# A decoder layer on one core: the value projections first, the first context's splits queued behind single units

## The chip, the cores and the metric

The kernel runs on one core of one Trainium2 chip. The metric is the device time of the whole program in microseconds (us). Before the change it is 2504.05 us, the median of three runs between 2503.03 and 2505.15.

## What is computed

One decoder layer over x (8 sequences of 100 tokens, 1024 wide) and a context of 8 x 722 vectors of 1024, all in float32:

```python
x = layernorm(x + retention(x))        # 8 heads, query/key 128, value 256, RoPE, decay, gate
x = layernorm(x + attention(x, ctx))   # 16 query heads, 4 key/value heads of 128
x = layernorm(x + ffn(x))              # SwiGLU, 4096 hidden

# attention(x, ctx): the part that the change touches
q, k, v = x @ wq, x @ wk, x @ wv                  # 16, 4 and 4 heads
q, k = rope(rms_norm(q)), rope(rms_norm(k))
k_ctx, v_ctx = rms_norm(ctx @ wk_ctx), ctx @ wv_ctx
out = softmax(q @ [k_ctx, k].T * scale + causal_mask) @ [v_ctx, v] @ wo
```

## The kernel before

**Tiles.** Activations lie with the feature on the partitions. The 800 tokens are two halves of N = 400 (four sequences each). A weight tile is 1024 x 128, held as 128 partitions x 1024. For float32 accuracy every operand is split into a high and a low part (`split2`, L60 to L68): ACT casts the high part, DVE subtracts it from the source for the low one, so each split is one ACT and one DVE instruction, both with line 68. One product is three matmuls (`mm3`, L90 high x high, L93 high x low, L94 low x high). `proj` makes one unit: 8 x 3 = 24 matmuls of 128 x 400 into one PSUM bank. There are eight banks: three with the tag "a" (projections), four "s", one "v".

**Places.** A tile gets the next place of its tag, in rotation, and waits until the tile that had it is done with. Raw weights have three places ("wst"), split weights four ("w"). `load_w` (L70 to L80) loads a raw weight (SP, L74) and splits it. `load_ws` (L82 to L85) loads a weight that was split earlier and stored (`wcd`, 1 MB, SP L84) straight into one of the same four "w" places.

**Order.** Each engine (PE, ACT, DVE, POOL, and SP, which here only issues DMAs) runs a fixed list of instructions, in which semaphores make it wait. The lists are laid out by a scheduler when the program is built, from the program's order, its dependences and a model of durations. Some things are pinned: `keep_in_program_order`, the function `todo` that `proj` calls between two of its matmul groups, and `tc.issue_after(i)`, which keeps an instruction behind instruction i on its engine.

**Stages.** Retention for eight heads; its output projection with the first layer norm (`out_proj`, "ln1"); the second projections ("l2", the changed loop); attention over eight sequences ("cx"); its output projection with the second norm; the feed-forward with the third.

**The norm ahead of the loop.** The second half's norm (`norm_late`, `inv_root`, `scaled`) is called from `todo` inside the last matmul groups of half 1's output and inside the first unit of the second projections, which uses half 0 only. Its sums over features are matmuls with a constant matrix (L291). On DVE it is: subtract (L343, L348), root (L133, L135), eight scalings (L312) and eight low parts of z (L68, z<-y,z); on ACT eight high parts of z.

**The second projections (L668 to L700).** For each kv head: units i = 0 to 3 are its four queries, 4 its key, 5 its value. Groups of a kv head are (0,4), (4,6) for the first and (0,2), (2,4), (4,6) for the others; in a group first the weights are loaded, then all units of half 0 and then those of half 1 run.

- A query or key unit: square (ACT L691), sum over partitions (POOL L140), rotation (`rope`: two ACT copies L148 and L149, three DVE products and sums L150 to L152, of which L150 reads the "a" bank), root of the mean (`inv_root`: ACT L127, L130, L132, DVE L133, L135), a DVE product (L696), a split into d (three places) and a store (SP L700, to qd or kd).
- A value unit: `tokens_first` copies the bank (ACT L160, one place "vt"), PE transposes four 100-token pieces into an "s" bank (L163), `split2` writes them into "vs" (one place) and SP stores that (L688, to vd, 100 partitions).

**The first context.** `load_context(0)` is called at the start of the second group. It loads eight pieces (SP L634, cs, into the weights' "wst" places) and splits each into two tiles with the tag "big" (ACT and DVE L68, big<-cs). The scheduler has put their splits between the instructions of the norm. `context_keys(kv)` loads a context key weight (`load_ws`) and returns `step`, which makes one half of the keys: 24 matmuls, a square, a POOL sum, a scaled copy and its low part. Steps for kv 0 and 1 run at the start of the groups (1,2), (2,0), (2,2) and (3,0); the attention's first sequence uses what they made.

Of the kernel before, what the change touches and what calls it, by code (L numbers as in the profile page):

```python
# [8 lines left out]
F32 = mybir.dt.float32  # L9
FR = mybir.dt.float32r  # L10
AF = mybir.ActivationFunctionType
ALU = mybir.AluOpType
# [4 lines left out]
P = 128  # L17
B, T, D = 8, 100, 1024
NB = 4
N = NB * T  # L20
KT = D // P
QT = KT // 2
# [9 lines left out]
NKV = 4  # L32
# [8 lines left out]
def decoder_layer(ctx, tc, xT, cT, w1, wo1, w2, wo2, wc, w3, wd, gw, qw, kw, trig, dec, mask, out):  # L41
    nc = tc.nc

    def sbuf(name, bufs, side=None):
        return tc.tile_pool(name=name, bufs=bufs, side=side, reuse_waits="tile")
# [8 lines left out]
    def bank(tag):  # L54
        return ps.tile([P, 512], F32, tag=tag, name=tag, bufs=banks[tag])

    def f32(ap):
        return ap.bitcast(F32)

    def bt(ap):  # L60
        return ap.rearrange("p (b t) -> p b t", b=NB)

    def split(dst, src):

        return split2(dst[:, 0], dst[:, 1], src)

    def split2(hi, lo, src):
        return nc.scalar.copy(hi, src), nc.vector.tensor_tensor(lo, src, f32(hi), ALU.subtract)  # L68

    def load_w(src, w=None, pinned=None):  # L70
        st = wp.tile([P, KT * P], F32, tag="wst", name="wst", bufs=3)
        if w is None:
            w = wp.tile([P, 2, KT * P], FR, tag="w", name="w", bufs=4)
        nc.sync.dma_start(out=st, in_=src)  # L74
        if pinned:
            with tc.issue_after(pinned[0].ins), tc.issue_after(pinned[1].ins):
                split(w, st)
        else:
            split(w, st)
        return w  # L80
# [32 lines left out]
    def proj(w, z, n=N, tag="a", todo=None):  # L113
        acc = bank(tag)[:, :n]
        for k in range(KT):
            pinned = between(todo, k)
            t = z[k // QT]
            mmw(acc, w, k, t[:, 0, k % QT, :n], t[:, 1, k % QT, :n], k == 0, k == KT - 1, pinned)
        return acc
# [4 lines left out]
    def inv_root(pool, ss, eps, n=N, pin=False, at=None):  # L124

        r = pool.tile([P, n], F32, tag="r0", name="r0") if at is None else at
        ln = nc.scalar.activation(r, ss, AF.Ln, bias=eps)  # L127
        if pin:
            tc.keep_in_program_order(ln)
        nc.scalar.activation(r, r, AF.Exp, scale=-0.5)  # L130
        q = pool.tile([P, n], F32, tag="r1", name="r1")
        nc.scalar.activation(q, r, AF.Square)  # L132
        nc.vector.scalar_tensor_tensor(q, ss, eps, q, ALU.add, ALU.mult)  # L133
        out = q if at is None else at
        nc.vector.scalar_tensor_tensor(out, q, 3.0, r, ALU.subtract, ALU.mult)  # L135
        return out

    def all_red(pool, x, tag, op=RED.add):
        y = pool.tile([P, N], F32, tag=tag, name=tag)
        nc.gpsimd.partition_all_reduce(y, x, P, op)  # L140
        return y

    def rope(pool, acc, cosw, sinw, tag="t1", op=ALU.add, swapped=None):

        t1 = pool.tile([P, N], F32, tag=tag, name=tag)
        t2 = pool.tile([P, N], F32, tag="t2", name="t2") if swapped is None else swapped
        h = P // 2
        nc.scalar.copy(t2[0:h], acc[h:P])  # L148
        nc.scalar.copy(t2[h:P], acc[0:h])  # L149
        nc.vector.tensor_tensor(bt(t1), bt(acc), cosw[:, None, :].to_broadcast([P, NB, T]), ALU.mult)  # L150
        nc.vector.tensor_tensor(bt(t2), bt(t2), sinw[:, None, :].to_broadcast([P, NB, T]), ALU.mult)
        nc.vector.tensor_tensor(t1, t1, t2, op)  # L152
        return t1

    def tokens_first(pool, acc, copied=True):

        vt = acc
        if copied:
            vt = pool.tile([P, N], F32, tag="vt", name="vt", bufs=1)
            nc.scalar.copy(vt, acc)  # L160
        tr = bank("s")
        for b in range(NB):
            nc.tensor.transpose(tr[0:T, b * P:(b + 1) * P], vt[:, b * T:(b + 1) * T], ident)  # L163
        return tr[0:T]
# [447 lines left out]
    with sbuf("ln1", 1) as p:  # L612
        z1, todo = [], None
        for half in range(2):
            todo, _ = out_proj(half, wo1, load_o1, xT, p, 2, p, lambda _: [
                z1p.tile([P, 2, QT, N], FR, tag="z", name="z") for _ in range(2)], zd, z1, todo)
        ws2 = [load_w(w2[0, 0])]
        acc2 = [proj(ws2[0], z1[0], todo=todo)]


# [1 line left out]
    ka = kapool.__enter__()  # L622
    cz = []

    def load_context(b):

        cz.clear()
        for hf in range(2):
            n = SN[hf]
            z = [big([P, 2, QT, SH]) for _ in range(2)]  # L630
            for k in range(0, KT, 2):
                cs = wp.tile([P, KT * P], F32, tag="wst", name="cs", bufs=3)
                cs = cs[:, :2 * n].rearrange("p (k n) -> p k n", k=2)
                nc.sync.dma_start(out=cs, in_=cT[b, :, k:k + 2, hf * SH:hf * SH + n])  # L634
                split(z[k // QT][:, :, k % QT:k % QT + 2, :n], cs)
            cz.append(z)

    def context_keys(kv):

        kall = ka.tile([P, 2, SC + T], FR, tag="kall", name="kall")  # L640
        wk = load_ws(2 * kv)
        sq = ka.tile([P, SC], F32, tag="ksq", name="ksq", bufs=1)
        ss = ka.tile([P, 6 * P], F32, tag="kss", name="kss", bufs=1)
        row = dr.tile([6, P], F32, tag="row", name="row", bufs=2)
        nc.gpsimd.memset(ss[:, SC:], 1.0)

        def step(hf):
            n, at = SN[hf], slice(hf * SH, hf * SH + SN[hf])
            acc = proj(wk, cz[hf], n)
            nc.scalar.activation(sq[:, at], acc, AF.Square)  # L650
            nc.gpsimd.partition_all_reduce(ss[:, at], sq[:, at], P, RED.add)  # L651
            nc.scalar.activation(kall[:, 0, at], acc, AF.Copy, scale=kws)
            nc.vector.scalar_tensor_tensor(kall[:, 1, at], acc, kws, f32(kall[:, 0, at]), ALU.mult, ALU.subtract)
            if hf:
                nc.sync.dma_start(out=row.rearrange("c p -> (c p)")[None, :], in_=ss[0:1])
        return step, (kall, row)
# [8 lines left out]
        return vt  # L665


    early = []  # L668
    with sbuf("l2", 2) as p:
        for kv in range(NKV):  # L670
            for i0, i1 in ((0, 4), (4, 6)) if kv == 0 else ((0, 2), (2, 4), (4, 6)):
                if (kv, i0) == (0, 4):
                    load_context(0)
                ws = [ws2.pop() if ws2 else load_w(w2[kv, i]) for i in range(i0, i1)]
                if (kv, i0) in ((1, 2), (2, 2)):
                    step, kept = context_keys(kv - 1)
                    early.append(kept)
                if (kv, i0) in ((1, 2), (2, 0), (2, 2), (3, 0)):
                    step(i0 == 0)
                for half in range(2):  # L680
                    bs = slice(half * NB, (half + 1) * NB)
                    for i in range(i0, i1):
                        acc = acc2.pop() if acc2 else proj(ws[i - i0], z1[half])
                        if i == 5:
                            tr = tokens_first(p, acc).rearrange("p (b d) -> p b d", b=NB)
                            vs = p.tile([T, NB, 2, P], FR, tag="vs", name="vs", bufs=1)
                            split2(vs[:, :, 0], vs[:, :, 1], tr)
                            nc.sync.dma_start(out=f32(vd[kv, :, bs]), in_=f32(vs))  # L688
                            continue
                        sq = p.tile([P, N], F32, tag="sq", name="sq")  # L690
                        nc.scalar.activation(sq, acc, AF.Square)  # L691
                        ss = all_red(p, sq, "ss")
                        tb = tq if i < 4 else tk
                        t = rope(p, acc, tb[:, 0], tb[:, 1], swapped=bank("s")[:, :N])
                        r = inv_root(p, ss, eps_k, at=bank("s")[:, :N])
                        nc.vector.scalar_tensor_tensor(  # L696
                            t, t, -0.5 if i < 4 else -0.5 * math.sqrt(P), r, ALU.mult, ALU.mult)
                        d = p.tile([P, NB, 2, T], FR, tag="d", name="d", bufs=3)
                        split2(d[:, :, 0], d[:, :, 1], bt(t))
                        nc.sync.dma_start(out=f32(qd[kv, i, :, bs] if i < 4 else kd[kv, :, bs]), in_=f32(d))  # L700
    z1pool.__exit__(None, None, None)


# [501 lines left out]
```

## Time and profile before

| | |
|---|---|
| median of three runs | 2504.05 us |
| profiled execution | 2504.06 us |
| its span, first to last instruction | 2502.3 us |
| granted TensorE clock, mean | 0.994 |
| PE busy | 2463.2 us (98%) |
| DVE busy | 1954.5 us (78%) |
| ACT busy | 1343.0 us (54%) |
| POOL busy | 464.8 us (19%) |

All times inside the program count from the span's start. The profile has several views: busy time of each engine in stretches of the span, with the granted clock of TensorE (1.00 is full speed) and the share that the DMA engines were busy; rows of waits (engine and line that waited, what ended the wait, total us, how often, the longest); a timeline of instructions (start, duration, engine, line, operation, output<-inputs, shape, how many in a row, and in brackets the idle time ahead of it); and the chain of work that ended last. "SPq" rows are DMAs that SP issued. The norm and the second projections lie between about 577 and 860 us.

### The profile page before, as it was taken

How to read it: one execution, taken by the hardware profiler on the slowest of the kernel's cores; microseconds unless marked ns; L12 is line 12 of the kernel's file. 1: busy time of each engine (PE TensorE's matmuls, PEld its weight loads, DVE VectorE, ACT ScalarE, POOL GpSimd, SP SyncE). 2: the span in 40 equal slices, each digit the busy share in tenths (PEclk: the TensorE clock that was granted, in tenths of full speed). 3: DMA queues.
4: the chain of work that ended last, by engine and by line, in shares of the span. 5: the costliest groups of instructions: out<-in, count | busy, mean ns of one | idle time of the engine just before them, and what ended most of it. 6: DMA issues, size and time to landing. Idle time of an engine off the chain costs nothing.

```text
span 2502.3 us, 37231 instructions
## 1 busy us (share of the span) xinstructions
PE 2463.2 (98%) x14068; PEld 2440.7 (98%) x14068; DVE 1954.5 (78%) x3101; ACT 1343.0 (54%) x2260; POOL 464.8 (19%) x234
## 2 busy tenths in 40 slices
PE   9999999997999999999999999999999999999997
PEld 9999999997999999999999999999999999999997
DVE  7778877567877688989999999866987777666756
ACT  6666676335767555656566666533544544432221
POOL 0111111002455343433433434100000000000000
PEclk9999999998999999999999999999999999999999
DMA  7333445774444654554554553574445444389731
GB/s 242 111 111 128 137 144 178 242 271 134 166 145 137 210 174 160 163 167 155 167 176 142 168 195 127 199 256 153 143 175 195 169 166 168 124 285 324 276 103 53
DMA packets 224451, 433.98 MB, mean 173 GB/s; under 512 B 47338, under 2 KB 168042, under 8 KB 211854
## 3 DMA queue, kind: packets, MB, share of 16 engines
q1 hardware_dynamic: 222542, 426.87, 50.2%
q0 software_dynamic: 1152, 4.19, 1.1%
q8 instruction: 111, 1.82, 0.3%
q14 instruction: 70, 0.57, 0.1%
q10 hardware_dynamic: 576, 0.52, 0.1%
HBM read 322.18 MB, written 109.35 MB: 172 GB/s over the span
## 4 chain that ended last, share of the span: by engine, by line
PE 93%; DVE 3%; DMA 2%; ACT 1%; issue 1%; POOL 0%; SPq 0%; DVEq 0%; ACTq 0%
PE a L94 20%; PE a L90 20%; PE a L93 20%; PE s L94 9%; PE s L93 9%; PE s L90 9%; PE v L94 2%; PE v L90 2%; PE v L93 2%; PE s L531 1%; PE s L734 1%; PE s L163 1%; DVE w L68 1%; DMA big<-o1d 1%; DVE y L312 0%
## 5 line engine op out<-in xcount | busy, mean ns | idle before, releaser
L90 PE MATMUL a<-big,w 128*128 128x400 f32 (+2 forms) x1808 | 609.5, 338 | 2.8 <-DMA w<-wcd 1.0
L93 PE MATMUL a<-big,w 128*128 128x400 f32 (+2 forms) x1808 | 609.3, 337 | 0.3 <-DVE big L68 0.3
L94 PE MATMUL a<-big,w 128*128 128x400 f32 (+2 forms) x1808 | 607.6, 337 | 0.4 <-DVE w L68 0.4
L68 ACT CAST w<-wst 128x1024 fp32r<-128x1024 f32 (+1 forms) x231 | 239.6, 1039 | 397.4 <-PE a L94 144.0
L68 DVE TENSOR_TENSOR w<-wst,w 128x1024 fp32r<-128x1024 f32 (+1 forms) x231 | 284.6, 1232 | 143.0 <-ACT w L68 141.7
L90 PEld LDWEIGHTS a<-big,w 128*128 128x128 f32 x1808 | 339.7, 188 | 5.9 <-ACT big L68 1.7
L93 PEld LDWEIGHTS a<-big,w 128*128 128x128 f32 x1808 | 340.3, 188 | 1.9 <-DVE big L68 1.0
L94 PEld LDWEIGHTS a<-big,w 128*128 128x128 f32 x1808 | 340.2, 188 | 1.2 <-DVE w L68 0.6
L90 PE MATMUL a<-z,w 128*128 128x400 f32 x680 | 236.4, 348 | 17.7 <-DVE t L150 16.0
L94 PE MATMUL a<-z,w 128*128 128x400 f32 x680 | 236.1, 348 | 0.0
L93 PE MATMUL a<-z,w 128*128 128x400 f32 x680 | 236.0, 347 | 0.0
L90 PE MATMUL s<-big,w 128*128 128x400 f32 x664 | 231.7, 349 | 2.4 <-ACT w L68 1.8
L94 PE MATMUL s<-big,w 128*128 128x400 f32 x664 | 229.9, 347 | 1.0 <-DVE w L68 1.0
L93 PE MATMUL s<-big,w 128*128 128x400 f32 x664 | 229.8, 346 | 0.0
L140 POOL PARTITION_ALL_REDUCE ss<-sq x56 | 150.7, 2693 | 328.8 <-DMA zd<-y 167.8
L651 POOL PARTITION_ALL_REDUCE kss<-ksq x64 | 166.7, 2604 | 127.8 <-ACT ksq L650 127.2
L90 PEld LDWEIGHTS a<-z,w 128*128 128x128 f32 x680 | 128.7, 189 | 19.5 <-DVE t L150 13.3
L768 ACT ACTIVATE s<-s,rk 128x400 f32<-128x400 f32 x160 | 87.9, 592 | 95.4 <-DVE sm L788 65.4
L90 PEld LDWEIGHTS s<-big,w 128*128 128x128 f32 x664 | 125.0, 188 | 5.3 <-ACT w L68 3.0
L94 PEld LDWEIGHTS a<-z,w 128*128 128x128 f32 x680 | 129.4, 190 | 0.0
L93 PEld LDWEIGHTS a<-z,w 128*128 128x128 f32 x680 | 128.7, 189 | 0.5
L94 PEld LDWEIGHTS s<-big,w 128*128 128x128 f32 x664 | 125.7, 189 | 1.7 <-DVE w L68 1.7
(356 smaller groups left out, 5443.8 us busy)
## 6 DMA issues: line engine op xcount, KB each, us to landing
wst<-in_w SPq DMA_DIRECT2D x135, 512.0 KB
w<-wcd SPq DMA_DIRECT2D x64, 1024.0 KB
wst<-in_wo SPq DMA_DIRECT2D x64, 512.0 KB
hd<-h SPq DMA_DIRECT2D x12, 1400.0 KB
wst<-in_wd SPq DMA_DIRECT2D x64, 256.0 KB
big<-o1d SPq DMA_DIRECT2D x16, 800.0 KB
qd<-d SPq DMA_DIRECT2D x32, 400.0 KB
q<-qd SPq DMA_DIRECT2D x32, 400.0 KB
```

What stands on the lines that cost most here:

```text
L68: return nc.scalar.copy(hi, src), nc.vector.tensor_tensor(lo, src, f32(hi), ALU.subtract)
L90: i = nc.tensor.matmul(acc, lh, rh, start=start, stop=False, skip_group_check=chain)
L93: nc.tensor.matmul(acc, lh, rl, start=False, stop=False, skip_group_check=chain)
L94: nc.tensor.matmul(acc, ll, rh, start=False, stop=stop, skip_group_check=chain)
L140: nc.gpsimd.partition_all_reduce(y, x, P, op)
L163: nc.tensor.transpose(tr[0:T, b * P:(b + 1) * P], vt[:, b * T:(b + 1) * T], ident)
L531: nc.tensor.matmul(bt(o)[:, b], vv[:, b * P:(b + 1) * P], pf[:, b], start=True, stop=True)
L651: nc.gpsimd.partition_all_reduce(ss[:, at], sq[:, at], P, RED.add)
L734: nc.tensor.transpose(tr[0:rows, (c - c0) * P:(c - c0 + 1) * P], vt[:, c * P:c * P + rows], ident)
L768: nc.scalar.activation(sc, sp, AF.Copy, scale=rk[:, c:c + 1])
```

## The change

- The first weight loaded is the value weight of kv head 0, not its first query's.
- The loop runs over a flat list of groups: first all four values (eight units: four with half 0, four with half 1), then for each kv head the group of queries 0 and 1 and the group of queries 2, 3 and the key.
- `load_context` becomes a generator, `context_steps`, that makes one of its eight pieces at each call. The first context's pieces are asked for one by one ahead of units 4 to 11 (counted from 0), so from the first value of half 1 on. They have two places of their own in the pool of the loop, and `issue_after` puts the split of a piece behind the split of the latest unit, on ACT and on DVE.
- The steps of the context's keys stand at the start of groups 2, 3, 5 and 7 (counted from 0).

Later contexts are loaded as before. In the built program the instruction lists of all engines are the same ahead of the norm and from the attention's first part on; between 577 and about 950 us they differ in order, with the same matmuls.

```diff
-        ws2 = [load_w(w2[0, 0])]
+        ws2 = [load_w(w2[0, 5])]
...
-    def load_context(b):
+    def context_steps(b, pool, bufs, behind=None):
...
-                cs = wp.tile([P, KT * P], F32, tag="wst", name="cs", bufs=3)
+                cs = pool.tile([P, KT * P if behind is None else 2 * SH], F32, tag="wst", name="cs", bufs=bufs)
                 cs = cs[:, :2 * n].rearrange("p (k n) -> p k n", k=2)
                 nc.sync.dma_start(out=cs, in_=cT[b, :, k:k + 2, hf * SH:hf * SH + n])
-                split(z[k // QT][:, :, k % QT:k % QT + 2, :n], cs)
-            cz.append(z)
+                to = z[k // QT][:, :, k % QT:k % QT + 2, :n]
+                if behind is None:
+                    split(to, cs)
+                else:
+                    with tc.issue_after(behind[0].ins), tc.issue_after(behind[1].ins):
+                        split(to, cs)
+                if k == 0:
+                    cz.append(z)
+                yield
+
+    def load_context(b):
+        for _ in context_steps(b, wp, 3):
+            pass
...
     early = []
+    behind = [None, None]
+    groups = [[(kv, 5) for kv in range(NKV)]]
+    for kv in range(NKV):
+        groups += [[(kv, i) for i in range(2)], [(kv, i) for i in range(2, 5)]]
+    unit = 0
     with sbuf("l2", 2) as p:
-        for kv in range(NKV):
-            for i0, i1 in ((0, 4), (4, 6)) if kv == 0 else ((0, 2), (2, 4), (4, 6)):
-                if (kv, i0) == (0, 4):
-                    load_context(0)
-                ws = [ws2.pop() if ws2 else load_w(w2[kv, i]) for i in range(i0, i1)]
-                if (kv, i0) in ((1, 2), (2, 2)):
-                    step, kept = context_keys(kv - 1)
-                    early.append(kept)
-                if (kv, i0) in ((1, 2), (2, 0), (2, 2), (3, 0)):
-                    step(i0 == 0)
+        ctx0 = context_steps(0, p, 2, behind)
+        for g, group in enumerate(groups):
+            ws = [ws2.pop() if ws2 else load_w(w2[kv, i]) for kv, i in group]
+            if g in (2, 5):
+                step, kept = context_keys(len(early))
+                early.append(kept)
+            if g in (2, 3, 5, 7):
+                step(g in (3, 7))
+            for half in range(2):
+                bs = slice(half * NB, (half + 1) * NB)
+                for (kv, i), w in zip(group, ws):
+
+                    if 4 <= unit < 12:
+                        next(ctx0)
+                    acc = acc2.pop() if acc2 else proj(w, z1[half])
+                    unit += 1
+                    if i == 5:
...
+                        behind[:] = split2(vs[:, :, 0], vs[:, :, 1], tr)
...
+                    behind[:] = split2(d[:, :, 0], d[:, :, 1], bt(t))
```

More of the change, by code (lines that the diff above doesn't have):

```diff
@@ L668, in decoder_layer @@
     early = []
-    with sbuf("l2", 2) as p:
-        for kv in range(NKV):
-            for i0, i1 in ((0, 4), (4, 6)) if kv == 0 else ((0, 2), (2, 4), (4, 6)):
-                if (kv, i0) == (0, 4):
-                    load_context(0)
-                ws = [ws2.pop() if ws2 else load_w(w2[kv, i]) for i in range(i0, i1)]
-                if (kv, i0) in ((1, 2), (2, 2)):
-                    step, kept = context_keys(kv - 1)
-                    early.append(kept)
-                if (kv, i0) in ((1, 2), (2, 0), (2, 2), (3, 0)):
-                    step(i0 == 0)
[L680 to L700, printed above, removed]
@@ new lines, in decoder_layer @@
+    behind = [None, None]
[3 more added lines that the diff above has]
+    unit = 0
+    with sbuf("l2", 2) as p:
+        ctx0 = context_steps(0, p, 2, behind)
[14 more added lines that the diff above has]
+                    if i == 5:
+                        tr = tokens_first(p, acc).rearrange("p (b d) -> p b d", b=NB)
+                        vs = p.tile([T, NB, 2, P], FR, tag="vs", name="vs", bufs=1)
+                        behind[:] = split2(vs[:, :, 0], vs[:, :, 1], tr)
+                        nc.sync.dma_start(out=f32(vd[kv, :, bs]), in_=f32(vs))
+                        continue
+                    sq = p.tile([P, N], F32, tag="sq", name="sq")
+                    nc.scalar.activation(sq, acc, AF.Square)
+                    ss = all_red(p, sq, "ss")
+                    tb = tq if i < 4 else tk
+                    t = rope(p, acc, tb[:, 0], tb[:, 1], swapped=bank("s")[:, :N])
+                    r = inv_root(p, ss, eps_k, at=bank("s")[:, :N])
+                    nc.vector.scalar_tensor_tensor(
+                        t, t, -0.5 if i < 4 else -0.5 * math.sqrt(P), r, ALU.mult, ALU.mult)
+                    d = p.tile([P, NB, 2, T], FR, tag="d", name="d", bufs=3)
+                    behind[:] = split2(d[:, :, 0], d[:, :, 1], bt(t))
+                    nc.sync.dma_start(out=f32(qd[kv, i, :, bs] if i < 4 else kd[kv, :, bs]), in_=f32(d))
```

## The prediction

> **What bounds the kernel now.** Read the page's busy shares first: PE is busy 98% of the span, the slices show one stretch with a lower digit inside the kernel (slice 10, 563 to 626 us), and the chain of waits is 93% PE. So the end moves only by what changes PE's idle time, or its clock, around the second projections. The table by stretches says where (columns: window, us, PE, PEld, DVE, ACT and POOL busy, granted clock, DMA share, GB/s).
>
> ```profile
> 580.00:600.00 20.00, 18.64 (x98) 17.42 (x96) 18.33 (x31) 11.91 (x20) 0.00 (x0) 1.00 0.53 154
> 600.00:610.00 10.00, 0.00 (x0) 0.00 (x0) 9.93 (x20) 7.42 (x15) 1.71 (x1) 0.61 0.76 275
> 610.00:620.00 10.00, 8.34 (x35) 8.30 (x36) 6.52 (x14) 5.91 (x13) 8.33 (x3) 0.71 0.00 0
> 620.00:630.00 10.00, 8.82 (x49) 8.52 (x48) 9.93 (x15) 8.62 (x17) 5.65 (x3) 1.00 0.25 91
> 630.00:640.00 10.00, 6.97 (x30) 6.60 (x30) 9.97 (x15) 7.12 (x14) 5.39 (x2) 0.83 0.52 181
> 800.00:820.00 20.00, 20.00 (x112) 20.00 (x111) 19.16 (x36) 16.92 (x35) 11.33 (x6) 1.00 0.49 158
> ```
>
> PE stands still from 598.6 to 611.7, loses 1.3 and 3.2 us more by 635.8, and runs at half clock behind two of these stops; from 640 to 860 it is full but for about 0.9 us. The wait rows name the engine, and DVE's timeline why it is late:
>
> ```profile
> PE a L90 <- DVE t L150: 16.0, 2, 13.0
> PE a L90 <- DMA w<-wcd: 1.0, 2, 0.6
> ```
> ```profile
> 603.26 3.97 DVE L312 SCALAR_TENSOR_TENSOR y<-y,r 128x400 f32<-128x400 f32 x8
> 607.15 3.97 DVE L68 TENSOR_TENSOR z<-y,z 128x400 fp32r<-128x400 f32 x8
> 611.03 0.57 DVE L150 TENSOR_TENSOR t<-a,tq 128x400 f32<-128x400 f32 x1
> ```
>
> The first query's L150 must read its "a" bank, and on DVE it stands behind the eight scalings and eight splits of the LN1 norm; all three "a" banks are held, so PE waits 13.0 us.
>
> **Part 1, gained in the norm.** The eight splits of the first context (L68, big<-cs) leave the norm for later places: 8 x 0.91 = 7.3 us of DVE between 576 and 602, some of it also waiting for ACT's half, which waits for the loads. The norm without such guests is in this trace too, in LN2: its variance matmul starts at 1739.86, its first scaling (L312) at
>
> ```profile
> 1745.10 3.98 DVE L312 SCALAR_TENSOR_TENSOR y<-y,r 128x400 f32<-128x400 f32 x8
> ```
>
> so 5.24 us lie between. In LN1 the variance matmul starts at 596.04; walked without the context's splits it starts at 594.0 (DVE frees the inputs earlier and the sum is 5 matmuls further up PE's order). 594.0 + 5.24 = 599.25: the scalings come 4.0 us earlier.
>
> **Part 2, gained behind the norm.** The first unit is now a value. What PE waits for is ACT's copy (L160), not DVE's L150: ACT's eight z casts (603.87 to 607.7 now) end near 603.7, the copy takes 0.49, PE transposes at 604.4. PE's stop is 598.75 to 604.4 = 5.65 instead of 13.0. It is still long enough for the clock to fall, as the 3.2 us stop shows at 630 to 640 (clock 0.83; some ten matmuls at 0.333 instead of 0.181 us, 1.5 us); I leave 1.7 us for it, as before. The values behind it need no DVE work ahead of their bank's release, so the stops of 1.3 and 3.2 us and the second slow clock go. Idle and slow clock from 580 to 660 sum to 18.25 + 3.2 = 21.4 us now and to 5.65 + 1.7 = 7.35 then: 14.1 gained. Walked by points: the twelfth unit ends at 659.85 now; eight values among twelve units carry seven more sets of four transposes (0.44 each) = 3.1; the new twelfth unit (query 1 of half 1) ends at 648.4. 659.85 + 3.1 - 648.4 = **14.5**; I take 14.4. The transposes are only moved, not added.
>
> **Part 3, lost at the first context key step.** A step now stands directly behind the twelfth unit. Its weights (w<-wcd, 1 MB) rotate through the same four places: with three weights loaded ahead of it in the group, it takes the place of the query weight that the twelfth unit has just read. Before, two were loaded ahead of it, and one whole unit (4.36 us) lay between the place's release and PE's use; that cover is gone. The chain shows what it was:
>
> ```profile
> 673.42 0.02 issue
> 673.44 4.77 DMA w<-wcd
> 678.21 0.14 issue
> 678.34 0.40 PE a L90
> ```
>
> Here the load takes 4.77 + 0.14 us, so even an immediate issue stops PE for 4.9. I don't expect an immediate one. SP issues in its order, and ahead of this load stands a weight load that waits for the DVE half of the split of the tile in its place; that split stands behind the values' and the context's splits. And the values' splits are slow as a row: "vs" has one place, so value u's cast waits until value u-1's store has landed. Two values that follow each other show it now:
>
> ```profile
> 779.24 0.30 SPq L688 DMA_DIRECT2D vd<-vs  x1
> ```
> ```profile
> 784.67 0.59 ACT L68 CAST vs<-s 100x512 fp32r<-100x512 f32 x1 [2.82 <-DMA vd<-vs]
> ```
>
> The store issued at 779.24 lets the next cast go at 784.67, 5.4 us later. The eight stores of this trace land 3.66 to 5.33 us after issue, one at 6.99 in heavy traffic (844). A period is cast 0.59 + DVE 0.69 + landing: 4.9 to 6.6 us for these, against PE's 24 x 0.1815 + 0.44 = 4.8 for a value. So ACT and DVE fall behind PE at each value, and all that is queued behind them. The second store of each of the four pairs, with least beside it, took 4.57, 5.20, 3.66 and 4.84 (mean 4.57). I walk the five landings between values 3 and 8 with a mean of 4.6 (the first at 6.0 because weight loads run beside it, the last at 3.8): casts at 616.5, 623.8, 629.4, 634.8, 640.8, 645.8. Behind the last, ACT still has a context split (0.80), a query's d and rows, and a weight cast: 651.5; DVE's half ends at 652.9; SP issues that weight load, then w<-wcd at 653.3; beside it the 512 KB load costs some 1.2 us: landed at 659.2. PE stops from 648.4 to 659.2 = **10.9** with what lies around the issue, plus 1.7 of slow clock, less the 0.9 us that the old steps lost. Net -11.7.
>
> **DMA rule and row.** The trace has the same 400 KB stored from 128 rows (queries' qd) in 2.4 us, from 100 rows (vd) in 3.66 to 5.33. The Trainium skill, "DMA: Bandwidth & Descriptors", section "Why a DMA increments its semaphore by 16 and not by 1", gives a reason that speaks against the change: a transfer uses the largest number of engines up to 16 that divides its outer size, so 100 rows use 10 engines. If value stores went like the queries', a period would be 0.59 + 0.69 + 2.4 = 3.7 us, below PE's 4.8, the stop would be 4.9, and the time 2496; by the row it is the sum below.
>
> **Part 4, the rest.** From 660 on, units are queries and keys: ACT and DVE spend 4.1 to 4.2 us on one and PE 4.36; nine in a row at 780 to 826 keep PE full (window 800 to 820 above), an eight-unit stretch with four weight splits took 4.8. So the long rows hold nearly, and the context's own places (two, no longer the weights' three) take its loads from the weights' rotation. The second context weights have a unit of cover, as before. The last unit is now a key, whose store the mask work of the attention waits for. Bounds: a gain of 1 (no weight load late) and a loss of 4 (eight units at 0.4); I take a loss of **1**, nearer to the full row at 800.
>
> **Sum.** 14.4 - 11.7 - 1.0 = 1.7 us gained, against the profiled execution's 2504.06 (span 2502.3), which is the median of 2504.05: 2502.3, rounded to **2502**. A difference of 0.2% (5 us) is about what a measurement of this kernel can tell from no change.
>
> **Rivals.**
> 1. The stores land early, faster. With 3.66 each the last cast comes 5 x 0.92 = 4.6 us earlier, at 641.2, w<-wcd goes out at 648.7 and PE stops 6.3 us: gain 6.3, 2498. With SP not late at all the stop is 4.9 and the gain 7.7: 2496.4. For it: SP has little else, and the cast order leaves slack wherever a store is quick. Against: seven of the eight rows are at 4.57 or more.
> 2. The chain of the single place takes over, slower. Five landings stand in a row ahead of the context weights, so each us over 4.57 costs 5 us. At 5.33, the slowest undisturbed row, the sum is a loss of 2.1 (2506); from 5.9 on it is slower by over 5; at 6.3 it is 2511. For it: context loads now run beside these stores, and the store in traffic took 6.99. Against: these loads are one 362 KB transfer per 5 us, and three of the four second stores took 3.66 to 4.84.
> 3. The change gives back what it takes: the norm's gain is there in full and lost at the context weights. That is my forecast, 2502; if the clock stays full at either stop, 1.7 better.
>
> **How the numbers follow.** Forecast (within 0.2%, 2499 to 2509) 0.46; rival 1 (faster) 0.29; rival 2 (slower) 0.25. The range runs from the stop at its least (2496) to landings of 6.3 (2511), which leaves about 0.2 outside.
>
> **What the changed profile would show.** Right: PE's stop near 600 is 5 to 6 us and ends on ACT's copy; the L150 waits of 16.0 are gone; a row of PE waiting for w<-wcd of about 10 us at 648 to 660; ACT's casts of vs waiting several us for vd<-vs. Wrong: no such w<-wcd wait over 5 us; PE stops among the values; a late L150 of the first query (I have it at 643.5, and PE wants its bank at 643.9: no slack); idle time behind 700 or at the attention's start over 2 us.

## The result

The change makes the kernel slower: 2509.15 us, the median of 12 runs (2507.86 to 2514.13), against 2504.25 us before (12 runs, 2503.0 to 2505.67). The ratio is 1.0023, with a 95% interval of 1.0015 to 1.0031. Forecast were 2502 us, a gain of about 2, in a range from 2496 to 2511; measured is a loss of 4.9.

The profiled execution took 2508.3 us, its span 2506.5: 4.2 more than the 2502.3 before. These are its stretches, with the same columns as before:

```profile
590.00:600.00 10.00, 7.87 (x40) 6.94 (x38) 7.15 (x15) 3.11 (x6) 0.00 (x0) 1.00 0.06 23
600.00:610.00 10.00, 6.52 (x30) 6.43 (x31) 6.96 (x15) 4.40 (x10) 0.00 (x0) 0.66 0.84 275
610.00:620.00 10.00, 10.00 (x61) 9.89 (x60) 2.52 (x3) 3.04 (x6) 0.00 (x0) 1.00 0.31 82
...
650.00:660.00 10.00, 0.00 (x0) 0.00 (x0) 9.74 (x16) 8.96 (x18) 5.76 (x2) 0.58 0.87 305
660.00:670.00 10.00, 9.18 (x42) 9.20 (x43) 5.28 (x10) 2.67 (x5) 2.38 (x1) 0.74 0.28 110
...
740.00:750.00 10.00, 7.35 (x35) 7.05 (x34) 7.95 (x15) 6.51 (x13) 2.63 (x2) 0.83 0.73 258
```

PE now works again from 603.5 on and is full from 610 to 648, where before it had three stops. But the whole of 650 to 660 is empty, and 740 to 750 has a new gap. The wait rows of the changed kernel between 570 and 960:

```profile
PE a L90 <- DVE t L715: 12.5, 1, 12.5
PE s L163 <- ACT vt L160: 5.6, 1, 5.6
PE a L90 <- ACT s L130: 2.6, 1, 2.6
PE s L90 <- DVE s L783: 2.1, 1, 2.1
```

The second row is the stop in the norm: 5.6 us on ACT's copy, in place of 13.0 on DVE's L150. The first is the new one at 648. Its named releaser is a trap: the matmul waits for several things, and L715 (which was L696 before) is only the one that the profile puts last. Put PE's row beside SP's (PE first, then SP):

```profile
660.83 0.64 PE L90 MATMUL a<-big,w 128*128 128x362 f32 x1 [12.45 <-DVE t L715]
```
```profile
653.98 0.34 SPq L74 DMA_DIRECT2D wst<-in_w  x1
654.37 0.42 SPq L84 DMA_DIRECT2D w<-wcd  x1
```

The matmul is the first of a context key step, and its weights went out at 654.37. Their last completion event is at 660.69, so the load took 6.32 us, and PE starts 0.14 later, the same distance as in the chain of the kernel before. L715 ended 0.02 us ahead of PE's start, and what it writes is a query's tile that this matmul doesn't read. The weights ended the wait, not DVE. The third row has the same trap:

```profile
743.61 0.58 PE L90 MATMUL a<-big,w 128*128 128x362 f32 x1 [2.65 <-ACT s L130]
```

The weights of this second step were issued at 736.62 and their last event is at 743.48, again 0.13 ahead of PE. ACT's L130 ends at the same moment, so the times alone can't tell the two apart here; the first two experiments do. The fourth row is a wait of DVE that PE inherits:

```profile
861.12 0.37 DVE L783 SCALAR_TENSOR_TENSOR s<-s,msk 54x216 f32<-54x216 f32 x1 [7.43 <-DMA kd<-d]
```

By its semaphores the mask operation waits for the stores of the last three d tiles, so its own tile has taken over their places. The last of these stores is issued at 853.71 and lands at 860.99.

### The profile page after: what moved, and what is told of

Read it like the earlier page. It is cut to its first block, busy times and chain, and to the rows that moved or that the text cites. A ratio compares the mean times of both kernels' runs of the same rounds, so it can differ in the third digit from the quotient of the medians.

```text
span 2506.5 us, 37239 instructions
## 1 busy us (share of the span) xinstructions
PE 2463.1 (98%) x14068; PEld 2442.1 (97%) x14068; DVE 1951.8 (78%) x3101; ACT 1343.0 (54%) x2260; POOL 463.7 (18%) x234
## 4 chain that ended last, share of the span: by engine, by line
PE 93%; DMA 3%; DVE 2%; ACT 1%; issue 0%; SPq 0%; DVEq 0%; ACTq 0%
PE a L94 19%; PE a L90 19%; PE a L93 19%; PE s L94 9%; PE s L90 9%; PE s L93 9%; PE v L94 2%; PE v L90 2%; PE v L93 2%; PE s L531 1%; DMA vd<-vs 1%; PE s L753 1%; PE s L163 1%; DMA big<-o1d 0%; PE v L523 0%
## 5 line engine op out<-in xcount | busy, mean ns | idle before, releaser
L68 ACT CAST w<-wst 128x1024 fp32r<-128x1024 f32 (+1 forms) x231 | 239.6, 1038 | 402.9 <-PE a L94 143.1
L68 DVE TENSOR_TENSOR w<-wst,w 128x1024 fp32r<-128x1024 f32 (+1 forms) x231 | 281.5, 1219 | 144.8 <-ACT w L68 143.5
```

## The experiments

All times are medians, and the ratios are to runs of the kernel before on the same chip. Its medians there lie between 2503.53 and 2504.25, so a difference to the changed kernel, which is taken across chips, is open by some 0.7 us. **First: is it the weights or the late engines?** Two kernels, one that takes the single vs place away, one that gives the key weights a place released earlier.

```diff
-                        vs = p.tile([T, NB, 2, P], FR, tag="vs", name="vs", bufs=1)
+                        vs = p.tile([T, NB, 2, P], FR, tag="vs", name="vs", bufs=2)
```

> The changed kernel with two places for vs instead of one, so that a value's cast no longer waits for the store just before it. Theory (the context key weights set the first stop: their place is released by the twelfth unit, and SP's queue adds to it): ACT, DVE and SP are no longer late, so the load goes out as the twelfth unit ends (648.4) and the stop shrinks from 12.45 to about 5, with the slow clock behind it still there; second and third stop (2.65 and 2.1) unchanged: 2509.2 - 7.5 = 2501.7 us. Rival (the late chain of the single place is the whole cause, as the wait row that names DVE's L715 reads): the stop and its slow clock go, 2495 us.

Measured: 2507.86 us (ratio to before 1.0017, 1.0008 to 1.0026), 1.3 less than the changed kernel, not 7.5 or 14; the two intervals overlap, so not even this gain is shown. The wait rows now name the cause openly:

```profile
PE a L90 <- DMA w<-wcd: 11.8, 2, 9.0
PE s L163 <- ACT vt L160: 5.6, 1, 5.6
PE s L90 <- DVE s L783: 2.2, 1, 2.2
```

And SP's queue shows that one half of the theory held:

```profile
648.82 0.34 SPq L74 DMA_DIRECT2D wst<-in_w  x1
649.74 0.34 SPq L84 DMA_DIRECT2D w<-wcd  x1
650.17 0.38 SPq L719 DMA_DIRECT2D qd<-d  x1
650.67 0.38 SPq L634 DMA_DIRECT2D cs<-in_cT  x1
```

The engines were no longer late, and the load went out as soon as the twelfth unit had ended. But it took 8.83 us instead of 4.77, with three transfers issued within 1 us of it, so the stop is still 9.0. The chain of work shows it, with the same distance between the landing and PE:

```profile
649.74 8.83 DMA w<-wcd
658.57 0.14 issue
658.70 0.64 PE a L90
```

The rival falls: without the late chain the stop is there all the same.

```diff
-            ws = [ws2.pop() if ws2 else load_w(w2[kv, i]) for kv, i in group]
             if g in (2, 5):
                 step, kept = context_keys(len(early))
                 early.append(kept)
+            ws = [ws2.pop() if ws2 else load_w(w2[kv, i]) for kv, i in group]
```

> The changed kernel with each context key weight loaded ahead of its group's own weights, so that it takes a place that was released long before; vs keeps one place. Theory: the stops of 12.45 and 2.65 us at the two key steps go with their slow clocks (1.9 and 1.5); third stop stays: 2509.2 - 18.5 = 2490.7 us. Rival (the chain of the single place): ACT and DVE are still about 10 us behind at 648, so PE waits there for banks instead of weights (L150 of the queries at 649, 654 and 660), and only some 7 to 9 us are gained: 2501 us.

Measured: 2495.73 us (0.9967, 0.9955 to 0.998), 13.4 less than the changed kernel and faster than the kernel before. The first key weights are issued at 625.71, more than 20 us ahead of their use. They took 7.09 us there: the load is hidden, not faster. What PE still waits for:

```profile
PE s L163 <- ACT vt L160: 5.6, 1, 5.6
PE a L90 <- DVE kall L664: 1.8, 1, 1.8
PE a L90 <- DVE t L150: 1.5, 1, 1.5
PE s L90 <- DVE s L783: 1.4, 1, 1.4
```

Both stops on weights are gone, so the weights were their cause. The result lies midway between the theory (2490.7) and the rival (2501), and both have a share in it: 3.3 us of waits on DVE stand where the first stop was. Another part is told in the last section.

**Second: which part of the change costs?** Each part alone. The order of units with the context loaded as before:

```diff
-        ctx0 = context_steps(0, p, 2, behind)
         for g, group in enumerate(groups):
+            if g == 1:
+                load_context(0)
...
-                    if 4 <= unit < 12:
-                        next(ctx0)
```

> The changed kernel with the first context loaded as before the change (at the start of the second group, in the weights' places, its splits between the norm's instructions); the order of units is the changed one. Theory: the norm's scalings are 4 us late again, the chain of stores is unchanged in its pace (landings set it) but has no context splits in it, so SP is about 3 us earlier behind the norm: the stop at the first key step stays, 8 to 10 us; 2509 to 2511 us. Rival (the splits in the units are what costs): the first stop is at most 5, 2504 us or less.

Measured: 2512.42 us (1.0031, 1.0019 to 1.0043). The rows are as the theory has them: 9.7 us in the norm (the scalings late again, though the value needs less of DVE) and 12.0 on w<-wcd, 8.8 of it at the first step. The splits in the units are not what costs.

And the context's pieces alone, in the order of the kernel before (the generator, and ahead of each unit's `proj`):

```diff
-                if (kv, i0) == (0, 4):
-                    load_context(0)
...
+                        if 4 <= unit < 12:
+                            next(ctx0)
                         acc = acc2.pop() if acc2 else proj(ws[i - i0], z1[half])
+                        unit += 1
```

> The kernel before, with its order of units, but the first context's pieces queued one by one behind units 4 to 11, in two places of their own. Theory: the norm's scalings come 4 us earlier and the stop of 13.0 us shrinks to about 9; DVE has 4.17 + 0.91 us per unit against PE's 4.36, so some 0.7 us for each of eight units come back as waits for banks, and the stops of 1.3 and 3.2 grow: 2502 to 2506 us. The key steps keep their cover of one unit. Rival (the context's move alone is good, the order of units alone is bad): 2500 us or less.

Measured: 2503.61 us (1.0, 0.9991 to 1.0009), no change. The long stop shrinks from 13.0 to 9.0, as expected, but the waits on L150 only from 16.0 in two to 14.1 in three, and the waits for weights grow from 1.0 to 1.9. So the order of units carries the loss: 8.9 us when alone, and with it the context's move, worth nothing by itself, takes some of it back (4.9 us lost with both).

**Third: what is left when the weights come early.** With both edits of the first pair:

> Context key weights loaded first in their groups, and two places for vs. With one place and the weights first, PE still lost 1.5 us (L150) and 1.8 us (kall, L664) at 653 to 660. Theory: these two are the rest of the late chain of the single vs place, and go: 2495.7 - 3 = 2492.7 us. Rival: ACT and DVE are short of time by themselves there (a unit's 4.17 us and a context split's 0.91 on DVE against PE's 4.36), so they stay: 2495.5 us.

Measured: 2491.92 us (0.9955, 0.9942 to 0.9967). Theory: the two waits on DVE are gone, PE is full from 610 to 830, and only these wait rows are left:

```profile
PE s L163 <- ACT vt L160: 5.6, 1, 5.6
PE s L90 <- DVE s L783: 2.0, 1, 2.0
```

So the single place does set the pace of ACT and DVE; it was only hidden behind the weights. For the last row, the key was put ahead of the queries in the last group:

```diff
-        groups += [[(kv, i) for i in range(2)], [(kv, i) for i in range(2, 5)]]
+        groups += [[(kv, i) for i in range(2)], [(kv, i) for i in ((2, 3, 4) if kv < 3 else (4, 2, 3))]]
```

> Context key weights loaded first in their groups, and in the last group the key unit ahead of the two queries. Theory: the third stop (1.4 us in that kernel, 2.1 in the changed one) is the last key's store, issued late and landing among the attention's weight loads; with two units more it goes: 2495.7 - 1.4 = 2494.3 us. Rival: the last queries' stores land as late and the attention's loads of them take the stop over: 2495.7 us.

Measured: 2495.88 us (0.9969, 0.9957 to 0.9981): nothing gained, and the theory that the key's store, as a key's, is the cause falls. The wait of the mask operation is now put down to a query:

```profile
846.67 0.38 DVE L783 SCALAR_TENSOR_TENSOR s<-s,msk 54x216 f32<-54x216 f32 x1 [7.51 <-DMA qd<-d]
```

So it seems to be the last d store, whichever unit it belongs to. To test that, the last value was put last, as before the change, on top of the early weights and two vs places:

```diff
-    groups = [[(kv, 5) for kv in range(NKV)]]
+    groups = [[(kv, 5) for kv in range(NKV - 1)]]
...
-        groups += [[(kv, i) for i in range(2)], [(kv, i) for i in range(2, 5)]]
+        groups += [[(kv, i) for i in range(2)], [(kv, i) for i in (range(2, 5) if kv < 3 else range(2, 6))]]
```

> Context key weights first in their groups and two places for vs, and the value of the last kv head as the last unit instead of among the first eight, as before the change. Theory: the third stop (2.0 us and 1.5 us of slow clock in the kernel without this) depends on the last unit being one whose d store the attention's first mask operation waits for; with a value last it goes, as in the kernel before: 2491.9 - 3 = 2489 us. Rival: any store issued last lands 7 us later among the attention's loads and stops PE: 2492 us.

Measured: 2492.49 us (0.9954, 0.9942 to 0.9967). The third stop is gone (the mask operation waits 2.13 us, and PE not at all), so the stop does depend on the last d store, as the theory has it: the operation starts 0.12 us after that store has landed, but the store now goes out 5.0 us ahead of the first scores that the operation masks (833.00 against s<-q,kall at 838.03) instead of 0.8 us behind them (833.50 and 832.73). (In the kernel before it waits for the last value's store, which lands at 851.21, 0.09 ahead of it; which store counts depends on what lay in the place.) The time is the same, because six values among the first units instead of eight let a stop of 2.5 us on L150 open at 675, with slow clock behind it.

**Fourth: do the neighbours stretch the load?** Two vs places, weights not early, and the context's pieces 4 to 7 moved away:

```diff
-                    if 4 <= unit < 12:
+                    if 4 <= unit < 8 or 14 <= unit < 18:
```

> The changed kernel with two places for vs and the context's pieces 4 to 7 asked for at units 14 to 17 instead of 8 to 11, so that no context load lies beside the first context key weights. With two places alone, the weights went out at once (649.74) and took 8.83 us to land, with a weight load ahead, a query store and a context load behind. Theory (the transfers beside it stretch the landing): without the context load it takes 6 to 7 us, the first stop is 6.5 instead of 9.0: 2505.5 us. Rival (the load takes 8 to 9 whatever lies behind it): 2508 us.

Measured: 2511.24 us (1.0028, 1.0017 to 1.0039), a miss as a time: the later pieces come too late for the second half of the key step, with new stops of 2.3 and 2.2 us that end at 692.7 and 695.3 (waits for big, L68). The load itself, issued at 649.73, took 7.41 us instead of 8.83, so it was 1.4 us shorter without the context load. This isn't a clean price, for the query store moved too, from 0.4 us behind the load to 0.4 ahead, and in the same company, a weight load and a query store 0.9 and 0.4 us ahead, the second key load of the changed kernel took 6.86. The runs give this row of durations for one and the same 1 MB: 4.77 with nothing issued within 3 us of it, 6.32 with a weight load 0.4 us ahead and stores and context loads in flight, 6.86, 7.41 and 8.83 as above. The load is longer in every one of these rows that has company; how much each neighbour adds is not shown.

**Last: the best version, and the old order with the same aids.**

> All three edits together: context key weights first in their groups, two places for vs, the key ahead of the queries in the last group. Theory: all three stops behind the norm go, only the one at 600 (5.6 us and 1.7 of slow clock) stays: 2491 to 2492 us. Rival: what the single edits left comes back at another place: 2494 us or more.

Measured: 2489.65 us (0.9947, 0.9934 to 0.9959), the lowest median of this study, 14.4 us under the kernel before and 19.5 under the changed one. The interval overlaps with that of the kernel without the key's edit (0.9942 to 0.9967), so what that edit adds is not shown. PE is full from 610 to 840; at the attention's start 1.1 and 0.7 us stay.

> The order of units of the kernel before, with the context's pieces queued behind units (as in context_steps_only), context key weights first in their groups and two places for vs. Theory: in that order the key weights cost 1.9 us and the first queries' banks 14 us, so 2503.6 - 2 = 2501.5 us, and the order with the values first is worth some 10 us once its key weights are loaded first. Rival (the early weights and the second place help any order as much): 2492 us.

Measured: 2500.23 us (0.9986, 0.9977 to 0.9995). The waits on w<-wcd are gone here too, and 14.1 us on L150 stay. So the order with the values first is worth some 8 to 11 us once its key weights are early and vs has two places. Without these it costs 5 with the context's pieces queued behind units in both orders, and 9 with the context loaded as before.

## Why the prediction was wrong

- **Parts 1 and 2, the norm (14.4 us gained): right, within 0.7 us.** Predicted were scalings from 599.25, a stop of 5.65, slow clock of 1.7 us and the twelfth unit's end at 648.4. The trace has the scalings at 598.50, a stop of 5.61, and the twelfth unit's last matmul from 648.03 on with 0.34: 648.4. But this trace runs 0.75 us early before anything has changed: the norm's first matmul with the constant matrix (L335) starts at 577.94, and at 578.69 in the kernel before. Counted from there the scalings come just as walked, the twelfth unit ends 0.7 us late, and 13.8 us are gained where the bare points give 14.5. (The sum by idle time, with 18.25 us, was a second way to the same gain; the rows shown add up to 17.2.)
- **Part 3, the first key step (11.7 us lost): right in mechanism, about 1.6 short.** The casts of vs were walked at 616.5, 623.8, 629.4, 634.8, 640.8 and 645.8; ACT's rows have 616.00, 623.22, 629.72, 635.26, 640.97 and 646.40. The load went out at 654.37 (653.3 in the walk) and took 6.32 us (5.97; the 1.2 us in it for the weight load beside was a guess without a row, and 6.32 is 1.55 over 4.77). The stop was 12.45 instead of 10.9, the slow clock 1.9.
- **Part 4, "the rest" (1.0 us lost): this step failed.** It said that the second context weights have a unit of cover, as before, and that the attention waits for the last key's store, and put both into one bound, from a gain of 1 to a loss of 4. Measured were a second stop of 2.65 us with 1.5 of slow clock, and a third of 2.1 with 0.2: 6.45. The unit of cover was indeed there (the weights went out as the unit that held their place ended), but no duration was set against it, and the one row that the prediction shows, 4.77, is that of a load with nothing issued within 3 us of it. The kernel before had longer rows of the same load, with query stores beside it: 5.60 and 8.21 us for those issued at 815.01 and 819.38. With a weight load and a query store 0.9 and 0.4 us ahead it now took 6.86, and PE waited:

```profile
735.70 0.33 SPq L74 DMA_DIRECT2D wst<-in_w  x1
736.18 0.32 SPq L719 DMA_DIRECT2D qd<-d  x1
736.62 0.36 SPq L84 DMA_DIRECT2D w<-wcd  x1
```

- **The sum.** 13.8 gained; 12.45 + 1.9 lost at the first step, less the 1.0 of the old rows; 4.15 and 2.3 behind it: 6.0 lost by the attention. The forecast had 1.7 gained, so it is off by 7.7, of which 5.4 lie in part 4, 1.6 in part 3 and 0.6 in the norm. All these kernels have a mark, the end of a short stop of PE behind the attention (1663.22 before, 1668.99 after). From the matmul at 578.69 and 577.94 to this mark the changed kernel takes 6.5 us more, so 0.5 us stays unexplained. The spans differ by only 4.2: 0.75 is the head start, and 1.5 comes behind the mark, as the last section tells.
- **The rivals.** The second, slower through the chain of the single place, had the right sign for the wrong reason: the casts kept the walked pace, within 0.8 us, and no landing over 5.3 us was needed. The first (early landings) did not come: the five distances between a store and the next cast average 4.6 us, the value taken. That this value came out is in part luck. It rests on 4.84 us for the second store of the fourth pair, but 4.84 is the first one's; the second took 6.99, and with it the four average 5.1.
- **The DMA rule.** The changed trace agrees with the row, not with the stores as quick as the queries': from the store at 636.60 to the cast at 640.97 there are 4.4 us, and the store of 642.30 has 10 completion events as it lands (and one at its issue) where a 128-row store has 16. But what the period costs was not decisive: with two vs places the load was no longer late, and 9.0 of the 12.45 us were still there.

## What to carry to other kernels

When a loop is reordered, follow each rotating place through the new order: a tile takes the place of the one so many tiles back, and one more load ahead of it in a group can move the release from a unit earlier to the last unit itself. A cover of one unit is only as good as the load's duration in its real company; take it from a contended row, or load first what is used first, which turned this change from 4.9 us slower into 7.8 us faster, and into 14.4 us faster with the other two edits. Before two traces are compared at a mark, look how far apart they are ahead of the edit. Where a wait has several semaphores, read the landing of the DMA before believing the engine that is named.

## What the hardware showed unexpectedly

The clock does not fall after each short stop. Near 1663 every one of these kernels has the same stop of PE, 1.84 us. Before the change it costs slow clock, after it not:

```profile
1660.00:1665.00 5.00, 3.16 (x15) 2.82 (x14) 4.09 (x7) 2.82 (x6) 0.00 (x0) 0.87 1.03 401
1665.00:1670.00 5.00, 5.00 (x23) 5.00 (x22) 1.72 (x3) 1.02 (x2) 0.00 (x0) 0.78 1.03 405
```
```profile
1665.00:1670.00 5.00, 3.15 (x17) 2.81 (x16) 4.19 (x8) 2.76 (x5) 0.00 (x0) 1.00 1.03 401
1670.00:1675.00 5.00, 5.00 (x28) 5.00 (x28) 2.40 (x5) 1.08 (x2) 0.00 (x0) 1.00 1.03 405
```

The first fence is the kernel before, the second the changed one; the same stop and work, with clock 0.87 and 0.78 there and 1.00 here. From this mark to the end the kernel before takes 839.1 us and the changed one 837.5. The same 1.5 us come and go in the experiments without an edit near them: of the twelve kernels five have the clock at 1.00 in the 8 us from 2 us ahead of the mark and take 837.5 or 837.6 us to the end; seven have it at 0.79, of which six take 839.0 or 839.1 and the one with the weights first 840.1. The Trainium skill, "TensorE: Matmul & The Clock Gate", section "Part 1: The HAM clock gate (the "warmup" mystery)", has the clock halved after an idle window of about 3.4 us, in windows that run on their own. The rows differ in the length: slow clock followed a stop of 1.84 us in seven of twelve kernels, and those of 2.5 and 2.65 us too. That the windows run freely would fit its coming and going; no run here varied it. So 1.5 us of a difference between two traces can lie in this stop alone, and marks just ahead of the edit and just behind it give the sharper comparison.

One 1 MB load that took 4.77 us with nothing issued within 3 us of it took 8.83 us when three transfers were issued within 1 us: a load's duration in a trace belongs to that trace's traffic.
